# A Perceiver-style network on one core: the second block's convolution, running means and perceptron in four interleaved parts

## The chip, the cores and the metric

The kernel runs on one core of a Trainium2 chip. Five engines work side by side, each through its own queue in order: TensorE (PE, matmuls, with its weight loads PEld), VectorE (DVE), ScalarE (ACT), GpSimd (POOL) and SyncE (SP, which here issues transfers). The metric is the device time of one launch in microseconds (us), as the median of several runs. Everything is float32.

## The reference

Sixteen sequences of 64 positions and 256 features pass through four layers; each adds three parts to x: a cross-attention to a context, a mixer, and a feed-forward part. The change lies in the second layer (L1), from the mixer to the start of the feed-forward part:

```python
x = x + _L1_xattn_ref(_layernorm(x), ctx_768, ...)
x = x + _L1_attn_ref(_layernorm(x), ...)
x = x + _L1_ffn_ref(_layernorm(x), ...)

# _L1_attn_ref, on its input x
h = _ln(x, ln_conv_g, ln_conv_b)
x = x + causal_conv(h, conv_w, K=4, groups=4) + conv_b
h = _ln(x, ln_attn_g, ln_attn_b)
q, k, v = h @ Wq.T + bq, h @ Wk.T + bk, h @ Wv.T + bv
scale = arange(1, S + 1)
pooled_q = cumsum(q, axis=1) / scale
pooled_k = cumsum(pooled_q * k, axis=1) / scale
x = x + pooled_k * v
h = _ln(x, ln_boom_g, ln_boom_b)
h = gelu(h @ Wb.T + bb) @ Wu.T + bu          # 256 -> 1024 -> 256
return x + h

# _L1_ffn_ref: top-1 of 8 experts, 256 -> 1024 -> 256
probs = softmax(x @ router_W + router_b)
gates = one_hot(argmax(probs)) * probs
y = relu(x @ W1[e] + b1[e]) @ W2[e] + b2[e]
out = einsum('bse,besd->bsd', gates, y)
```

## The kernel before

The 1024 rows of x stay in `xs` as eight tiles of 128 rows (tokens) by 256 features. Layers run one after another; a scheduler orders the instructions of each engine when the program is built, except where `manual_schedule` keeps an engine in the order of the text. Each layer opens pools of its own for SBUF (`lp`) and PSUM (`ps_misc` for `misc()`, `lps` for larger tiles); a tile waits until the memory that it takes over is free. Weights are loaded on SP into a ring of two slots: `pack()` hands out the weights of the current step and starts the load of the next (`ahead`).

A normalisation of a tile (`norm_tile`, L150 to L161) takes statistics, aggregate and variance plus epsilon on DVE, the power -1/2 on POOL (L160), and is applied on DVE (L170). `norm` does it for all eight tiles and hands each to `transposed` (two PE transposes into one PSUM tile, L179) and to `put`, which evicts to the features-first layout.

`L1_attn` (L1473) runs stage by stage over all eight tiles: `norm_x` makes `htok` (tokens) and `hT` (features; this one is not read here); a second norm with its own scale and shift goes to the padded `hp` (L1487); the convolution is four shifted matmuls for each of two feature halves and two column halves of 512 (evicted on ACT, L1502); `add_by_features` transposes back and adds (L1511, L1514); a norm into `hT` (L1521); then for each column half and feature half the three projections into PSUM tiles of 512 columns, one buffer for each of q, k, v, and the running means on DVE as scans with a product by 1/position (L1540, L1541, L1555, L1557); added back; a third norm; POOL adds the result to `xs` (L1565); the perceptron for each column half as eight matmul groups of 512 columns with GELU on ACT (L1572), and per tile nine matmuls of 256 columns, the last with the bias row, added to `xs` by `add_to_x` (L89).

`L1_ffn` (L1347) normalises `xs` again (`norm_x`), writes the eight `htok` tiles to DRAM (`hs`, by `keep_row` on SP), makes router logits for all tiles into one PSUM tile, and routes all tiles in one call of `route`: softmax, largest expert, rank of each token among those of its expert (`ranks`: a running count `seen`, two matmuls), one-hot rows and columns for the table of tokens (L1118, L1120, one matmul each), gates. `blocks` turns the counts into up to 15 blocks of 128 tokens of one expert: `rows` (rows of the expert's weights, L1263) and `tokens`. After that call the text adds the gated expert biases `b2` tile by tile (a transpose of the gates, an eviction, one matmul, `add_to_x`). Each block gathers its weights (`wa`, `wb`, 1 MB each) and its token rows (`hb`) by indirect transfers that POOL issues (L1304), three blocks ahead, and runs two matmul groups (`ph`, `po`). The block count is read by all engines after four blocks.

The cross-attention before (`L1_xattn`) and the one after are unchanged.

Of the kernel before, what the change touches and what calls it, by code (L numbers as in the profile page):

```python
# [20 lines left out]
T = B * S  # L21
# [4 lines left out]
E = 8  # L26
# [16 lines left out]
class Net:  # L43
# [4 lines left out]
    def __init__(self, tc, a):  # L48
        self.tc, self.nc, self.a = tc, tc.nc, a
        self.flip = 0  # L50
        self.n_pT = 2
        self.spare_dve = False
        self.halves = None
        self.sb = None
        self.routed = None
# [957 lines left out]
    def gate(self, name, n=NT):  # L1013
        return (self.sb or self.lp).tile([128, n, E], F32, name=name)

    def over_experts(self, x, op, name, out=None):
        n = x.shape[1]
        r = (self.sb or self.lp).tile([128, n], F32, name=name) if out is None else out
# [61 lines left out]
    def keep_row(self, i):  # L1080

        self.nc.sync.dma_start(self.hs[1 + i * 128 : 1 + (i + 1) * 128], self.htok[:, i, :])

    def route(self, r, logits, first, weighed=None, among_chosen=False):
# [18 lines left out]
        at = pool.tile([128, k, n], F32, name="s_at")  # L1103
# [5 lines left out]
        row = pool.tile([128, k, n], F32, name="s_row")  # L1109
# [220 lines left out]
    def pack_L1_gate(self):  # L1330
        self.slot()
        w, row = self.load("L1f_rW"), self.load_row("L1f_rb")
        b2 = self.carve(E, D)
        self.nc.sync.dma_start(b2, self.a["L1f_b2"])
        return w, row, b2

# [10 lines left out]
    def L1_ffn(self):  # L1347
        nc = self.nc
        rw, rb, b2 = self.pack()
        self.norm_x()  # L1350
        self.routed = r = self.route_setup(1)
        for i in range(NT):
            self.keep_row(i)
        gates = self.gate("gates")
        for _ in self.route(r, self.gate_logits(rw, rb), 0, gates):
            pass
        self.rows, self.tokens = self.blocks(r, L1_BLOCKS)
        for i in range(NT):
            pg = self.misc([E, 128])
            nc.tensor.transpose(pg, gates[:, i, :], self.ident)  # L1360
            gT = self.lp.tile([E, 128], F32, tag="gT", bufs=2, name="gT")
            self.evict(gT, pg)
            po = self.misc([128, D])
            self.mm(po, [(gT, b2)])
            self.add_to_x(i, po)
# [103 lines left out]
    def pack_L1_boom(self):  # L1469
        self.slot()  # L1470
        return self.load("L1a_WbT"), self.load("L1a_WuT"), self.load_row("L1a_bu")

    def L1_attn(self):  # L1473
        nc = self.nc
        cv, wq, wk, wv = self.pack()
        self.norm_x()
        h0 = self.htok

        def work(i):
            return self.lp.tile([128, D], F32, tag="lnw", bufs=2, name="lnw")  # L1480

        hp = self.lp.tile([128, 2, B, S + 3], F32, name="hp")
        nc.gpsimd.memset(hp[:, :, :, 0:3], 0.0)

        def put_padded(i, ps):
            for c in range(2):
                nc.vector.tensor_scalar(  # L1487
                    hp[:, c, 2 * i : 2 * i + 2, 3:], ps[:, c, :].rearrange("p (b s) -> p b s", s=S),
                    self.col("L1a_lcg", c), self.col("L1a_lcb", c), ALU.mult, ALU.add,
                )  # L1490

        self.norm(h0, 1e-5, work, put_padded)
        x1 = self.lp.tile([128, NT, D], F32, name="x1")
        conv = self.lp.tile([128, 2, T], F32, tag="res", name="conv")
        for half in range(2):
            for c in range(2):
                ps = self.lps.tile([128, 512], F32, tag="hid", bufs=2, name="ps_conv")
                self.mm(
                    ps.rearrange("p (b s) -> p b s", s=S),
                    [(cv[:, c, k, :], hp[:, c, half * 8 : half * 8 + 8, k : k + S]) for k in range(4)],  # L1500
# [805 lines left out]
```

## Time and profile before

| what | value |
|---|---|
| median of 3 runs (lowest, highest) | 3026.73 us (3026.29, 3029.28) |
| the profiled execution | 3029.32 us, span 3027.5 us |
| PE busy in the span | 2704.1 us (89%) |
| DVE, ACT, POOL busy | 1482.0, 1022.6, 309.4 us |
| mean granted TensorE clock | 0.942 |
| 998.44 to 1189.40: PE, DVE, ACT, POOL busy | 152.48, 96.67, 23.32, 32.35 of 190.96 us |
| granted clock there | 0.82 |

A busy PE is not one at its peak: matmuls are pipelined and their ends are modelled. A float32 matmul shows as two records (passes). The granted clock is the share of TensorE's full clock that was granted in a stretch. An engine's busy share over the whole span mixes stages with different limits; what a change in one stage is worth is read in that stage.

### The profile page before, as it was taken

Reading aid. Unit: us, or ns where it says so; the run is one execution under the profiler, and the core shown is the slowest. Engines: PE = TensorE matmul, PEld = TensorE weight load, DVE = VectorE, ACT = ScalarE, POOL = GpSimd, SP = SyncE. Lnnn points to the kernel's source line nnn. Section 1 sums busy time; section 2 is a strip of 40 time slices with the busy share of each in tenths; the row PEclk is TensorE's granted clock in tenths of the full one; section 3 lists DMA queues with packets and bytes.
Section 4 is the critical chain, followed back from the end, with each engine's and each line's share of the span. In section 5 each row is a group of like instructions: output and inputs, shape, how many; then the busy total and the mean of one; then the engine's idle time right before and its main releaser. Section 6 shows DMA issues by size and latency. Waiting matters only on the chain.

```text
span 3027.5 us, 42618 instructions
## 1 busy us (share of the span) xinstructions
PE 2704.1 (89%) x16840; PEld 1955.0 (65%) x16840; DVE 1482.0 (49%) x3177; ACT 1022.6 (34%) x2290; POOL 309.4 (10%) x428
## 2 busy tenths in 40 slices
PE   7888997999999787979999997887998898887899
PEld 3566784666666346857777776874766666665668
DVE  3654115666666643234444344223445657658581
ACT  2331122555555111223333321122335455455330
POOL 1112223000000112310101011201001000000000
PEclk9997997999999897989999998998999999998999
DMA  9504771101010004811111113450212212121110
GB/s 242 171 27 159 253 230 51 36 26 36 26 36 22 28 9 171 281 49 54 55 44 47 60 42 116 163 217 22 67 43 84 74 51 83 56 67 53 57 36 7
DMA packets 79220, 253.55 MB, mean 84 GB/s; under 512 B 15151, under 2 KB 26954, under 8 KB 69290
## 3 DMA queue, kind: packets, MB, share of 16 engines
q1 hardware_dynamic: 59562, 165.01, 17.5%
q0 software_dynamic: 13312, 80.28, 7.8%
q10 hardware_dynamic: 6144, 5.51, 0.5%
q8 instruction: 134, 2.20, 0.3%
q14 instruction: 68, 0.56, 0.1%
HBM read 233.80 MB, written 14.82 MB: 82 GB/s over the span
## 4 chain that ended last, share of the span: by engine, by line
PE 64%; DVE 11%; ACT 4%; DMA 3%; issue 3%; POOL 1%; SPq 1%; ACTq 0%; DVEq 0%; POOLq 0%
PE misc L69 11%; PE sc L500 8%; PE halves L69 7%; PE gu L69 5%; PE misc L235 4%; PE ps_h L69 4%; PE po L69 4%; PE ps_t L235 3%; PE sc L69 2%; PE misc L864 2%; ACT p L225 2%; PE o L915 2%; PE misc L878 2%; DMA back<-ys,route_at 2%; DVE x L1926 2%
## 5 line engine op out<-in xcount | busy, mean ns | idle before, releaser
L223 DVE TENSOR_REDUCE nmx<-sc 128x1 f32<-128x1024 f32 x264 | 311.6, 1218 | 234.9 <-PE sc L500 150.4
L225 ACT ACTIVATE p<-sc,nmx 128x1024 f32<-128x1024 f32 x264 | 294.6, 1116 | 312.1 <-DVE nmx L223 311.4
L500 PE MATMUL sc<-ctxT,qp 128*128 128x512 f32 (+1 forms) x1024 | 353.4, 599 | 0.0
L500 PEld LDWEIGHTS sc<-ctxT,qp 128*128 128x128 f32 (+1 forms) x1024 | 137.8, 189 | 153.0 <-issue 151.6
L69 PE MATMUL halves<-ctx,pT 128*128 128x192 f32 x1024 | 191.0, 343 | 9.4 <-DVE xs L89 4.0
L69 PEld LDWEIGHTS halves<-ctx,pT 128*128 128x128 f32 x1024 | 178.4, 203 | 12.3 <-DVE xs L89 4.5
L160 POOL TENSOR_TENSOR ln_rs<-ln_ve,nhalf 128x1 f32<-128x1 f32 x120 | 67.0, 563 | 1142.3 <-DVE ln_ve L158 1081.6
L69 PE MATMUL misc<-ctx,pT 128*128 128x192 f32 x1024 | 177.6, 327 | 0.5 <-DVE qT L465 0.5
L69 PEld LDWEIGHTS misc<-ctx,pT 128*128 128x128 f32 x1024 | 166.3, 191 | 2.1 <-DVE qT L465 1.0
L235 PE MATMUL ps_t<-ident,p 128*128 128x128 f32 x1088 | 147.2, 277 | 21.9 <-ACT p L225 14.0
L1916 ACT ACTIVATE da<-rep,al 128x252 f32<-128x252 f32 x256 | 114.7, 498 | 115.0 <-DVE x L1926 95.6
L1926 DVE TENSOR_TENSOR_SCAN x<-da,x 128x512 f32<-128x512 f32 x128 | 151.9, 1210 | 1.9 <-ACT da L1916 1.4
L235 PE MATMUL misc<-ident,p 128*128 128x128 f32 x1024 | 139.8, 283 | 14.1 <-ACT p L225 6.7
L237 ACT COPY pT<-ps_t 128x512 f32<-128x512 f32 x182 | 104.3, 585 | 139.3 <-PE ps_t L235 137.3
L235 PEld LDWEIGHTS ps_t<-ident,p 128*128 128x128 f32 x1088 | 127.1, 143 | 36.0 <-ACT p L225 17.7
L235 PEld LDWEIGHTS misc<-ident,p 128*128 128x128 f32 x1024 | 112.2, 143 | 40.2 <-ACT p L225 13.3
L69 PE MATMUL ps_h<-r,w 128*128 128x256 f32 x512 | 115.3, 385 | 0.0
L237 ACT COPY pT<-misc 128x512 f32<-128x512 f32 x128 | 75.0, 586 | 114.9 <-PE misc L235 114.6
L69 PEld LDWEIGHTS ps_h<-r,w 128*128 128x128 f32 x512 | 97.8, 192 | 16.6 <-issue 2.9
L69 PE MATMUL gu<-dT,wa 128*128 128x128 f32 (+1 forms) x864 | 104.7, 280 | 3.7 <-ACT dT L64 2.4
L239 DVE COPY pT<-misc 128x512 f32<-128x512 f32 x128 | 88.2, 689 | 39.4 <-PE misc L235 28.9
L69 PE MATMUL po<-wb,hid 128*128 128x256 f32 (+1 forms) x440 | 105.9, 388 | 0.2 <-ACT hid L1380 0.2
(468 smaller groups left out, 4449.5 us busy)
## 6 DMA issues: line engine op xcount, KB each, us to landing
ctx<-in_ctx SPq DMA_DIRECT2D x48, 768.0 KB
ctxT<-in_ctxT SPq DMA_DIRECT2D x48, 512.0 KB
w<-in_L2f_W SPq DMA_DIRECT2D x24, 1024.0 KB
rep<-dus SPq DMA_DIRECT2D x256, 64.0 KB
ctxT<-in_ctxT SPq DMA_DIRECT2D x16, 768.0 KB
ctxT<-in_ctxT SPq DMA_DIRECT2D x96, 128.0 KB
ys<-yb ACTq DMA_DIRECT2D x40, 128.0 KB
bc_rep<-bcs SPq DMA_DIRECT2D x32, 128.0 KB
```

Source lines behind the costliest of these rows:

```text
L69: self.nc.tensor.matmul(out, lhsT, rhs, start=n == 0, stop=n == len(pairs) - 1)
L160: nc.gpsimd.tensor_tensor(rs, ve, self.nhalf, ALU.pow)
L223: self.nc.vector.tensor_reduce(nmx, sc, AX.X, ALU.max, negate=True)
L225: self.nc.scalar.activation(p, sc, AF.Exp, bias=nmx, accum_out=sums)
L235: self.nc.tensor.transpose(ps[:, u, :], p[:, at : at + 128], self.ident)
L237: self.nc.scalar.copy(pT[:, 4 * g : 4 * g + 4, :], ps)
L239: self.nc.vector.tensor_copy(pT[:, 0:4, :], ps)
L500: nc.tensor.matmul(sc[u][:, bass.ts(kh, 512)], qp[n][par][rows, h : h + 2, :].rearrange("p h q -> p (h q)"), ctx[0][rows, at], start=n == ...
L864: nc.tensor.matmul(ps[kh], wk[:, kh, cols], cT[:, bass.ts(kh, 512)], start=True, stop=False)
L878: nc.tensor.matmul(ps[kh][:, u, :], cT[:, 512 * kh + at : 512 * kh + at + 128], wv[:, 0, :], start=u == 0, stop=False,)
L1916: nc.scalar.activation(da[:, g, :, 1:], now[j][:, 0, :].rearrange("p (b s) -> p b s", s=S)[:, :, 1:], AF.Exp, scale=al[:, col : col + 1],)
L1926: nc.vector.tensor_tensor_scan(flat, da.rearrange("p g b s -> p (g b s)"), flat, 0.0, ALU.mult, ALU.add)
```

## The change

The mixer and the routing of the next layer are written as one generator `part(p)` for two tiles (256 columns), in four parts that take turns: each `yield` ends a piece, and the loop at the end runs one piece of each part in turn, with PE kept in that order. All matmuls that had 512 columns have 256. The unread `hT` of the first norm is gone. Projections are evicted to SBUF on ACT (q, k and v, with their biases) ahead of the products on DVE, which work in place. Every small matmul result goes through `misc()`, with eight PSUM buffers in this layer. Each part then normalises its tiles, stores their rows, makes its logits and routes its two tiles (the running count goes from part to part), and adds its gated expert biases; `blocks` comes after all of that. The router's weights and `b2` are loaded with the perceptron's; the next layer's weights (L2x) are started at the end of the stage. Small routing tiles get four buffers.

The added functions in full, with the removed text of `L1_attn` left out:

```diff
@@ -51,7 +51,7 @@
         self.n_pT = 2
         self.spare_dve = False
         self.halves = None
-        self.sb = None
+        self.sb, self.gate_bufs = None, 1
         self.routed = None
 
 
@@ -1011,11 +1011,11 @@
         return ps
 
     def gate(self, name, n=NT):
-        return (self.sb or self.lp).tile([128, n, E], F32, name=name)
+        return (self.sb or self.lp).tile([128, n, E], F32, bufs=self.gate_bufs, name=name)
 
     def over_experts(self, x, op, name, out=None):
         n = x.shape[1]
-        r = (self.sb or self.lp).tile([128, n], F32, name=name) if out is None else out
+        r = (self.sb or self.lp).tile([128, n], F32, bufs=self.gate_bufs, name=name) if out is None else out
         self.nc.vector.tensor_reduce(r, x, AX.X, op)
         return r, r.unsqueeze(2).to_broadcast([128, n, E])
 
@@ -1077,9 +1077,9 @@
             row.rearrange("p (d o) -> p d o", o=1), self.lanes[:1, :1].unsqueeze(1).to_broadcast([1, D, 1])
         )
 
-    def keep_row(self, i):
-
-        self.nc.sync.dma_start(self.hs[1 + i * 128 : 1 + (i + 1) * 128], self.htok[:, i, :])
+    def keep_row(self, i, x=None):
+        self.nc.sync.dma_start(self.hs[1 + i * 128 : 1 + (i + 1) * 128], self.htok[:, i, :] if x is None else x)
 
     def route(self, r, logits, first, weighed=None, among_chosen=False):
 
@@ -1100,13 +1100,13 @@
         rank()
 
         k = len(masks)
-        at = pool.tile([128, k, n], F32, name="s_at")
+        at = pool.tile([128, k, n], F32, bufs=self.gate_bufs, name="s_at")
         for m, to in zip(masks, (at[:, x] for x in range(k))):
             t = self.gate("s_t", n)
             nc.vector.tensor_tensor(t, place, self.region.unsqueeze(1).to_broadcast([128, n, E]), ALU.add)
             nc.vector.tensor_tensor(t, t, m, ALU.mult)
             self.over_experts(t, ALU.add, "", to)
-        row = pool.tile([128, k, n], F32, name="s_row")
+        row = pool.tile([128, k, n], F32, bufs=self.gate_bufs, name="s_row")
         nc.vector.tensor_scalar(row, at, 63.5, 1.0 / 128, ALU.subtract, ALU.mult)
         nc.vector.tensor_scalar(row, row, 12582912.0, None, ALU.add)
         nc.vector.tensor_scalar(row, row, 12582912.0, None, ALU.subtract)
@@ -1327,13 +1327,6 @@
         self.nc.scalar.copy(yb, po)
         self.nc.scalar.dma_start(self.ys[j * 128 : (j + 1) * 128, :], yb)
 
-    def pack_L1_gate(self):
-        self.slot()
-        w, row = self.load("L1f_rW"), self.load_row("L1f_rb")
-        b2 = self.carve(E, D)
-        self.nc.sync.dma_start(b2, self.a["L1f_b2"])
-        return w, row, b2
-
     def L1_block(self, j, own=""):
         w = self.lp.tile([128, 2 * 1024 + 8], F32, tag="wa" + own, bufs=1 if own else 3, name="wa")
         self.gather_rows(w, self.a["L1f_W1b"], self.rows[:, j : j + 1])
@@ -1346,23 +1339,8 @@
 
     def L1_ffn(self):
         nc = self.nc
-        rw, rb, b2 = self.pack()
-        self.norm_x()
-        self.routed = r = self.route_setup(1)
-        for i in range(NT):
-            self.keep_row(i)
-        gates = self.gate("gates")
-        for _ in self.route(r, self.gate_logits(rw, rb), 0, gates):
-            pass
-        self.rows, self.tokens = self.blocks(r, L1_BLOCKS)
-        for i in range(NT):
-            pg = self.misc([E, 128])
-            nc.tensor.transpose(pg, gates[:, i, :], self.ident)
-            gT = self.lp.tile([E, 128], F32, tag="gT", bufs=2, name="gT")
-            self.evict(gT, pg)
-            po = self.misc([128, D])
-            self.mm(po, [(gT, b2)])
-            self.add_to_x(i, po)
+        self.rows, self.tokens = self.blocks(self.routed, L1_BLOCKS)
         def block(j, own=""):
             w1, b1, w2 = self.L1_block(j, own)
             dT = self.block_tokens(j, own)
@@ -1468,115 +1446,175 @@
     def pack_L1_boom(self):
         self.slot()
...
+        boom = self.load("L1a_WbT"), self.load("L1a_WuT"), self.load_row("L1a_bu")
+        gate = self.load("L1f_rW"), self.load_row("L1f_rb")
+        b2 = self.carve(E, D)
+        self.nc.sync.dma_start(b2, self.a["L1f_b2"])
+        return boom, gate, b2
     def L1_attn(self):
         nc = self.nc
...
+        (cv, *qkv), ((wb, wu, bu), (rw, rb), b2) = self.pack(), self.pack(ahead=False)
+        self.lps_close()
+        routed, self.gate_bufs = self.route_setup(1), 4
+        later = self.later_steps(CHUNK)
+        def tokens(p, name):
+            return self.lp.tile([128, 2, D], F32, name=f"{name}{p}")
+        def features(p, name):
+            return self.lp.tile([128, 2, CHUNK], F32, name=f"{name}{p}")
+        def normalized(src, out):
+            for t in range(2):
+                mv, rs = self.norm_tile(src(t), 1e-5)
+                nc.vector.tensor_scalar(out[:, t, :], src(t), mv[:, 0:1], rs, ALU.subtract, ALU.mult)
+        def affine(x, t, to, g, b):
+            ps = self.transposed(x[:, t, :])
             for c in range(2):
...
+                nc.vector.tensor_scalar(to(c), ps[:, c, :], self.col(g, c), self.col(b, c), ALU.mult, ALU.add)
+        def added(x, to):
+            for t in range(2):
                 ps = self.misc([128, D])
                 for c in range(2):
...
+                    nc.tensor.transpose(ps[:, c * 128 : (c + 1) * 128], x[:, c, t * 128 : (t + 1) * 128], self.ident)
+                nc.vector.tensor_tensor(to[:, t, :], to[:, t, :], ps, ALU.add)
+        def part(p):
+            tiles = (2 * p, 2 * p + 1)
+            hp = self.lp.tile([128, 2, 4, S + 3], F32, name=f"hp{p}")
+            nc.gpsimd.memset(hp[:, :, :, 0:3], 0.0)
+            x1, w = tokens(p, "x1"), tokens(p, "lnw")
+            normalized(lambda t: self.xs[:, tiles[t], :], x1)
+            normalized(lambda t: x1[:, t, :], w)
+            yield
+            for t in range(2):
+                ps = self.transposed(w[:, t, :])
                 for c in range(2):
                     nc.vector.tensor_scalar(
...
+                        hp[:, c, 2 * t : 2 * t + 2, 3:], ps[:, c, :].rearrange("p (b s) -> p b s", s=S),
+                        self.col("L1a_lcg", c), self.col("L1a_lcb", c), ALU.mult, ALU.add,
                     )
...
+            yield
+            ps = self.misc([128, 2, CHUNK])
+            conv = features(p, "hTs")
+            for c in range(2):
+                self.mm(
+                    ps[:, c, :].rearrange("p (b s) -> p b s", s=S),
+                    [(cv[:, c, k, :], hp[:, c, :, k : k + S]) for k in range(4)],
                 )
...
+            for c in range(2):
+                nc.scalar.activation(conv[:, c, :], ps[:, c, :], AF.Identity, bias=self.col("L1a_conv_b", c))
+            yield
+            added(conv, x1)
+            w = tokens(p, "lnw")
+            normalized(lambda t: x1[:, t, :], w)
+            yield
+            hT = features(p, "hTs")
+            for t in range(2):
+                affine(w, t, lambda c: hT[:, c, t * 128 : (t + 1) * 128], "L1a_lag", "L1a_lab")
+            yield
+            q, k, v = (features(p, name) for name in "qkv")
+            for m, x, name in zip(qkv, (q, k, v), "qkv"):
+                ps = self.misc([128, 2, CHUNK])
+                for o in range(2):
+                    self.mm(ps[:, o, :], [(m[:, c, o * 128 : (o + 1) * 128], hT[:, c, :]) for c in range(2)])
+                for o in range(2):
+                    nc.scalar.activation(x[:, o, :], ps[:, o, :], AF.Identity, bias=self.col(f"L1a_b{name}", o))
+                if name != "k":
+                    yield
+            inv = self.inv_s.unsqueeze(1).unsqueeze(1).to_broadcast([128, 2, 4, S])
+            def running_mean(x):
+                for c in range(2):
+                    nc.vector.tensor_tensor_scan(x[:, c, :], later, x[:, c, :], 0.0, ALU.mult, ALU.add)
+                steps = x.rearrange("p c (b s) -> p c b s", s=S)
+                nc.vector.tensor_tensor(steps, steps, inv, ALU.mult)
+            running_mean(q)
+            nc.vector.tensor_tensor(q, q, k, ALU.mult)
+            running_mean(q)
+            nc.vector.tensor_tensor(v, v, q, ALU.mult)
+            yield
+            yield
+            added(v, x1)
+            w = tokens(p, "lnw")
+            normalized(lambda t: x1[:, t, :], w)
+            for t in range(2):
+                x = self.xs[:, tiles[t], :]
+                nc.gpsimd.tensor_tensor(x, x, x1[:, t, :], ALU.add)
+            yield
+            hT = features(p, "hTs")
+            for t in range(2):
+                affine(w, t, lambda c: hT[:, c, t * 128 : (t + 1) * 128], "L1a_lbg", "L1a_lbb")
+            yield
+            if p < 2:
+                g = self.act.tile([128, 8, CHUNK], F32, tag=("htok", "hT")[p], name="hid")
+            else:
+                g = self.lp.tile([128, 8, CHUNK], F32, name=f"hid{p}")
+            for m2 in range(4):
+                ps = self.misc([128, 2, CHUNK])
+                for u in range(2):
+                    m = 2 * m2 + u
+                    self.mm(ps[:, u, :], [(wb[:, c, m * 128 : (m + 1) * 128], hT[:, c, :]) for c in range(2)])
+                for u in range(2):
+                    m = 2 * m2 + u
+                    nc.scalar.activation(g[:, m, :], ps[:, u, :], AF.Gelu, bias=self.col("L1a_bb", m))
+                if m2 == 1:
+                    yield
+            yield
+            for t in range(2):
                 po = self.misc([128, D])
                 self.mm(
                     po,
                     [(g[:, m, t * 128 : (t + 1) * 128], wu[:, m, :]) for m in range(8)] + [(self.ones[:1, :], bu)],
                 )
...
+                self.add_to_x(tiles[t], po)
+                yield
+            o = tokens(p, "x1")
+            normalized(lambda t: self.xs[:, tiles[t], :], o)
+            for t in range(2):
+                self.keep_row(tiles[t], o[:, t, :])
+            yield
+            hT = features(p, "hTs")
+            for t in range(2):
+                self.evict(hT[:, :, t * 128 : (t + 1) * 128], self.transposed(o[:, t, :]))
+            yield
+            ps = self.misc([128, 2, E])
+            for t in range(2):
+                self.mm(
+                    ps[:, t, :],
+                    [(hT[:, c, t * 128 : (t + 1) * 128], rw[:, c, :]) for c in range(2)] + [(self.ones[:1, :], rb)],
+                )
+            gates = self.gate(f"gates{p}", 2)
+            for _ in self.route(routed, ps, tiles[0], gates):
+                yield
+            yield
+            gTs = []
+            for t in range(2):
+                pg = self.misc([E, 128])
+                nc.tensor.transpose(pg, gates[:, t, :], self.ident)
+                gTs.append(self.lp.tile([E, 128], F32, tag="gT", bufs=8, name="gT"))
+                self.evict(gTs[t], pg)
+            yield
+            for t in range(2):
+                po = self.misc([128, D])
+                self.mm(po, [(gTs[t], b2)])
+                self.add_to_x(tiles[t], po)
+            yield
+        with self.tc.manual_schedule(engines={mybir.EngineType.PE}):
+            parts = [part(p) for p in range(NC)]
+            while parts:
+                parts = [p for p in parts if next(p, parts) is not parts]
+        self.start_pack(self.at)
+        self.routed, self.gate_bufs = routed, 1
@@ -2110,7 +2148,7 @@
             "L0_ffn": (self.L0_ffn, []),
             "L1_xattn": (self.L1_xattn, [self.pack_L1_xattn]),
             "L1_attn": (self.L1_attn, [self.pack_L1_attn, self.pack_L1_boom]),
-            "L1_ffn": (self.L1_ffn, [self.pack_L1_gate]),
+            "L1_ffn": (self.L1_ffn, []),
             "L2_xattn_attn": (self.L2_xattn_attn, [lambda: self.pack_heads64("L2"), self.pack_L2_attn]),
             "L2_ffn": (self.L2_ffn, [self.pack_L2_gate] + [lambda e=e: self.pack_L2_expert(e) for e in range(E)]),
             "L3": (None, [lambda: self.pack_heads64("L3"), self.pack_L3_attn, self.pack_L3_ffn]),
@@ -2127,7 +2165,7 @@
                 if name == "L0_first" else nullcontext() as sb,
                 tc.tile_pool(name=f"sb_{name}", bufs=1, side=side, reuse_waits="tile") as self.lp,
                 tc.tile_pool(
-                    name=f"psm_{name}", bufs=3 if name == "L1_xattn" else 2, space=PSUM, reuse_waits="tile"
+                    name=f"psm_{name}", bufs={"L1_xattn": 3, "L1_attn": 8}.get(name, 2), space=PSUM, reuse_waits="tile"
                 ) as self.ps_misc,
             ):
                 self.sb = sb
```

## The prediction

> **What bounds the kernel now.** I read the page's chain that ended last, then the busy times cut into the stages that the change touches, then the timeline where stages meet.
>
> ```profile
> span 3027.5 us, 42618 instructions
> PE 64%; DVE 11%; ACT 4%; DMA 3%; issue 3%; POOL 1%; SPq 1%; ACTq 0%; DVEq 0%; POOLq 0%
> ```
>
> PE sets most of the end, yet the second block is not one thing. The busy times by stage (columns: length, busy time and instructions of each engine, granted clock, DMA):
>
> ```profile
> core 0: us, PE busy (x) PEld busy (x) DVE busy (x) ACT busy (x) POOL busy (x), PEclk, DMA share, GB/s
> 998.44:1010.00 11.56, 5.43 (x24) 2.69 (x24) 9.85 (x39) 1.49 (x4) 3.30 (x6) 0.77 0.48 182
> 1010.00:1027.60 17.60, 17.23 (x40) 7.89 (x41) 5.16 (x20) 2.06 (x3) 1.65 (x3) 0.86 0.00 1
> 1027.60:1039.40 11.80, 5.58 (x28) 3.06 (x27) 10.14 (x37) 0.69 (x1) 2.71 (x5) 0.83 0.00 0
> 1039.40:1067.70 28.30, 24.52 (x61) 10.39 (x60) 25.78 (x46) 4.03 (x5) 2.18 (x4) 0.95 0.00 1
> 1067.70:1081.10 13.40, 5.32 (x20) 2.75 (x21) 10.24 (x37) 0.00 (x0) 7.67 (x13) 0.57 0.00 1
> 1081.10:1096.50 15.40, 15.40 (x40) 7.07 (x39) 5.32 (x20) 4.81 (x7) 1.62 (x3) 0.93 0.00 1
> 1096.50:1144.40 47.90, 47.90 (x177) 31.97 (x175) 11.27 (x36) 6.19 (x9) 4.11 (x8) 1.00 0.06 21
> 1144.40:1158.80 14.40, 12.64 (x65) 11.16 (x64) 3.11 (x10) 2.77 (x5) 0.55 (x1) 0.74 0.47 159
> 1158.80:1172.20 13.40, 5.71 (x22) 4.64 (x22) 10.63 (x58) 0.26 (x1) 0.00 (x0) 0.50 0.00 1
> 1172.20:1189.40 17.20, 12.74 (x27) 5.16 (x27) 5.16 (x23) 1.02 (x4) 8.56 (x9) 0.50 0.87 319
> ```
>
> In order: the convolution's normalisation, convolution, second normalisation, projections with running means, third normalisation, perceptron (two rows), router logits, routing, gated biases. The normalisations belong to DVE, the perceptron to PE (47.90 of 47.90). Two things matter here. PE begins each matmul phase when half of its tiles are ready (conv at 1010, projections at 1039.4), the other transposes lying between its matmuls. And the last row is not waste: 319 GB/s of expert weights flow under it.
>
> One normalisation, in the timeline (start, length, engine, line):
>
> ```profile
> 1101.26 0.43 DVE L154 BATCH_NORM_STATS2 ln_st<-xs 128x6 f32<-128x256 f32 x1
> 1101.72 0.18 DVE L156 BATCH_NORM_AGGREGATE ln_mv<-ln_st 128x2 f32<-128x6 f32 x1
> 1101.94 0.15 DVE L158 TENSOR_SCALAR ln_ve<-ln_mv 128x1 f32<-128x1 f32 x1
> 1102.24 0.55 POOL L160 TENSOR_TENSOR ln_rs<-ln_ve,nhalf 128x1 f32<-128x1 f32 x1 [17.04 <-DVE ln_ve L158]
> 1102.82 0.41 DVE L170 TENSOR_SCALAR htok<-xs,ln_mv,ln_rs 128x256 f32<-128x256 f32 x1 [0.73 <-POOL ln_rs L160]
> ```
>
> From the variance on DVE, through POOL's power, to the application: 1102.82 - 1101.94 = 0.88 us that other DVE work must fill.
>
> **The change, part by part.** The sum goes against the profiled execution (span 3027.5, 3029.3 in all), which is 2.6 above the median 3026.7. The order in which the changed kernel is built has PE walk whole rounds: the transposes of parts 0 to 3, then the convolutions of parts 0 to 3, and so on. DVE is ordered by the scheduler, and its row order is known. I price that order with DVE paces of back-to-back rows: application 0.32, statistics 0.33, aggregate 0.09, variance 0.06, affine eviction 0.33.
>
> *First normalisation.* Both norms of all eight tiles now stand behind the preceding cross-attention; before, six applications ran under it (PE there 99.7 to 100 busy of each 100 us, so freeing them there gains nothing). A part's turn on DVE is 4 applications, 4 statistics, 4 aggregates, 4 variances, 2 evictions: 1.28 + 1.32 + 0.36 + 0.24 + 0.66 = 3.86; each application waits a further 0.34 or so for POOL (0.88 less the 0.5 of rows that the order puts in between), 5.24. Lead 0.93 + three turns of 5.24 + a last one of 3.57 + 0.65 for transposes = 20.9, and only then may the first convolution start, since PE's queue holds it behind part 3's transposes. Before: 11.6. **+9.3.** Gone are the 16 transposes and 8 evictions into hT, which lay in the first 4 us.
>
> *Convolution.* 64 passes of 256 columns at 0.214 (perceptron rows: 16 in 3.62, hence 16 of 4.27 with the bias row) = 13.7, plus a slow start. The first expert block's 32 passes took 6.33 against 3.84 for the next: 2.5 lost, at a granted clock of 0.50. So 16.2 against 17.6: **-1.4.** Matmuls of half the width cost nothing by themselves, as the weight loads (0.19 to 0.20) hide under 0.214; without that cover the perceptron's 128 passes alone would cost 25 more.
>
> [...]
>
> *Second normalisation.* Eight tiles of add 0.33, statistics, aggregate, variance, application = 1.13 each, 9.0; three affine evictions 1.0; POOL waits 0.5 a tile, 4.1; ends 1.1: 15.2. Before, 11.8, since the first projection went after four tiles. **+3.4.**
>
> *Projections and means.* First q 3.4 (slow clock) + ACT and hand-over 1.1; DVE means 4 x 1.9 (two half-length scans of 1.22/2 and a 0.69 product) = 7.6; then 4 x 3.1 = 12.4, and two adds 0.7: 25.2, PE's 20.6 under it. Before 28.3 (PE waited for its PSUM buffers). **-3.1.**
>
> *Third normalisation.* As the second, 15.3, because POOL's eight residual adds (0.73 each, L1565) now lie between its powers, for +2, while some work has already run. Before 13.4. **+1.9.**
>
> *Perceptron.* 27.4 + 8 x 4.27 + 2.5 = 64.1 against 63.3. **+0.8.** The running sum at the last perceptron matmul is +10.9.
>
> *From there to the first expert matmul*, before: 1190.52 - (1143.73 + 0.69) = 46.1.
>
> ```profile
> 1171.98 0.23 DVE L1263 TENSOR_SCALAR rows<-of,lane 128x15 int32<-128x15 f32 x1
> 1172.49 1.00 POOL L1304 DMA_INDIRECT wa<-in_L1f_W1b,rows  x1 [25.68 <-DVE first L1278]
> 1190.52 6.33 PE L69 MATMUL ph<-dT,wa 128*128 128x128 f32 x32 [0.46 <-ACT dT L64]
> 1201.04 3.84 PE L69 MATMUL ph<-dT,wa 128*128 128x128 f32 x32 [0.52 <-DVE dT L62]
> ```
>
> After: last tile's norm and transposes 5.1; logits 9.9 as before; then in DVE's order the maxima of parts 2 and 3 stand first, so all routing follows part 3's logits. It has 85 small operations (before, some 26), 16 one-hot rows at 0.21 and four table adds at 0.3: 85 x 0.13 + 3.4 + 1.2 + 1.0 of PE round trips = 16.6. (0.13: thirteen interleaved rows from 1171.71 to 1173.31.) Gate transposes 0.7. The eight bias matmuls, 2 x 0.43 at half clock, 0.9 each: 7.2. They now stand in PE's queue ahead of the block count, so count 0.9 and rows 2.0 come after them, and the gathers begin with nothing left to cover them. Of their latency no row is direct: the windows show 243, 366, 360, 201 GB/s over 2 us each from 1174, so block 0's 2.23 MB are in by 1181.5, 9.3 after the rows; +0.2. Sum 51.9. **+5.8.** The 14 blocks at 8.0 are unchanged: three are gathered ahead, and one follows each finished block.
>
> *Queues.* On SP the three router loads move ahead to the perceptron's weights, then come L2x's five (held until the projections free their slot), then eight row stores, 0.33 to 0.43 each to issue: all are out some 30 us before the gather that reads the rows. L2a's five loads wait for the slot that the bias matmuls free, with the block count's load behind them on SP; it is needed only after four blocks. Their 0.64 MB meet the first gather, 1.5 at 427 GB/s, which the gather's upper bound holds. On POOL the block gathers stand behind nothing but the residual adds and powers, long done.
>
> [...]
>
> Sum: 10.9 + 5.8 = 16.7; 3046.0 for the profiled execution, **3043** as a median.
>
> Bounds of what no row shows: routing pace 0.06 (variance row) to 0.26 (dependent row), -6/+11; POOL wait per normalisation 0.2 to the full 0.88 over 32 of them, -9/+13; bias matmuls 0.43 (full clock) to 1.22 (as measured), -4/+3; logits all fast or all slow, -3/+2; gather 7.0 (427 GB/s, the best window, after 1.8 of silence) to 14.8 (sharing with block 1), -2/+6; three slow starts at 1.2 to 3.5 each, -4/+3. I take the values nearest to rows of the same stage.
>
> **The rivals.** *The parts overlap in earnest (faster):* in my count PE idles about 36 us before the perceptron (15.6, 10, 10 in the three norms). If DVE's work on one part really hides under PE's on another, and two thirds of that go, 24, the time is 3043 - 24 = 3019. It decides from 17 hidden microseconds on. For: 1010 to 1027.6 shows both engines working so. Against: PE's fixed rounds and the DVE sum, which even without stalls fills the norms.
>
> *POOL's wait stays bare (much slower):* +13, 3056. For: 0.73 idle before L170 in the rows above. Against: four chains to interleave.
>
> *Tail no longer than before:* full clock in logits and biases (-7), gather at 7.0 (-2), a few short routing rows (-2): 3032, no clear change. Against: 0.50 granted all through 1158.8 to 1189.4.
>
> *The parts don't take turns:* DVE's order could have put part after part; it alternates, so this has no share.
>
> **How the numbers follow.** Forecast 61%, bare wait 15%, unchanged tail 14%, overlap 10%. A difference under 0.2%, 6 us, can't be told from none. Faster 9%, all of it overlap; same 11%, mostly the unchanged tail; slower 80%. The bounds, which seldom fall all on one side, give about -13/+15, and the range takes in the bare wait and half of the unchanged tail: 3029 to 3058.
>
> **What would show it.** Right: first convolution at about 1019 and last perceptron matmul at about 1155 in the profile; PE idle over 8 us ahead of each matmul phase; the first gather after the last bias matmul, and PE idle some 9 us behind it. Wrong: convolution before 1012, a granted clock near 1.0 in the norms, or weights moving before the bias matmuls.

## The result and the profile after

The changed kernel is slower. Its median is 3041.11 us over 20 runs (3034.94 to 3046.49); the kernel before, run beside it, has 3028.52 over 20 (3021.72 to 3039.17). The ratio is 1.0039, with a 95% interval of 1.0030 to 1.0048: some 12 us, with 9 to 14.5 inside the interval. The profiled execution took 3038.85 us, 9.5 more than that of before.

The first row of the changed kernel's chain that ended last:

```profile
PE 63%; DVE 11%; issue 4%; ACT 4%; DMA 4%; POOL 2%; SPq 1%; ACTq 0%; DVEq 0%; POOLq 0%
```

Against before, PE has one point less of the chain, and GpSimd, DMA and "issue" (where no releaser is seen) have one more each. That is a hint and no more; the stages tell it. Busy times of the changed kernel, cut at the same events as before the change (columns: length, busy time and instructions of each engine, granted clock, DMA share, GB/s):

```profile
core 0: us, PE busy (x) PEld busy (x) DVE busy (x) ACT busy (x) POOL busy (x), PEclk, DMA share, GB/s
998.92:1019.20 20.28, 5.26 (x17) 2.52 (x18) 16.12 (x72) 0.00 (x0) 7.60 (x14) 0.50 0.28 105
1019.20:1035.00 15.80, 15.80 (x65) 13.44 (x65) 2.00 (x7) 2.52 (x6) 0.00 (x0) 0.87 0.01 1
1035.00:1049.80 14.80, 6.50 (x33) 3.96 (x32) 11.21 (x46) 0.84 (x2) 4.40 (x8) 0.68 0.00 0
1049.80:1076.40 26.60, 24.29 (x110) 20.93 (x108) 24.61 (x47) 11.36 (x25) 1.61 (x2) 0.92 0.09 36
1076.40:1092.20 15.80, 5.76 (x21) 2.96 (x22) 11.74 (x45) 0.00 (x0) 9.12 (x15) 0.55 0.20 74
...
1155.30:1170.00 14.70, 13.02 (x65) 12.40 (x64) 3.53 (x14) 3.12 (x7) 0.81 (x2) 0.65 0.05 15
1170.00:1183.20 13.20, 9.68 (x42) 7.13 (x41) 12.11 (x109) 1.23 (x6) 0.00 (x0) 0.50 0.00 1
1183.20:1187.10 3.90, 3.90 (x18) 3.10 (x17) 3.17 (x8) 0.13 (x1) 0.00 (x0) 0.94 0.00 0
1187.10:1190.20 3.10, 0.55 (x3) 0.45 (x2) 2.84 (x19) 0.00 (x0) 0.00 (x0) 0.50 0.51 140
1190.20:1200.60 10.40, 0.66 (x3) 0.55 (x3) 0.91 (x8) 0.00 (x0) 7.68 (x9) 0.50 0.89 291
```

In order: first normalisation, convolution, second normalisation, projections and means, third normalisation; then, past the perceptron, logits, routing, gated biases, block count, first gather. The first row holds most of the loss: 20.3 us where before had 11.6. In the three rows of normalisations PE is busy 5.26, 6.50 and 5.76 of 20.28, 14.80 and 15.80, so it idles for 15.0 + 8.3 + 10.0 = 33 us there, where before had 6.1 + 6.2 + 8.1 = 20. The last row is PE idle under a gather that moves 291 GB/s.

Inside the second normalisation, DVE's timeline of the changed kernel (start, length, engine, line, operation, and in brackets the idle time before it with its releaser):

```profile
1043.17 0.13 DVE L158 TENSOR_SCALAR ln_ve<-ln_mv 128x1 f32<-128x1 f32 x1
1043.23 0.41 DVE L1487 TENSOR_TENSOR x<-x,misc 128x256 f32<-128x256 f32 x1
1044.04 0.41 DVE L1473 TENSOR_SCALAR lnw<-x,ln_mv,ln_rs 128x256 f32<-128x256 f32 x1 [0.40 <-POOL ln_rs L160]
...
1045.64 0.41 DVE L1473 TENSOR_SCALAR lnw<-x,ln_mv,ln_rs 128x256 f32<-128x256 f32 x1 [0.40 <-POOL ln_rs L160]
```

A tile takes 1.60 us (1044.04 to 1045.64), and 0.40 of it is the wait for GpSimd's power, tile after tile: DVE's order puts one row (0.41) between a variance and the application that needs it, and the round trip takes 0.87 (1043.17 to 1044.04).

The stretch runs from the last attention matmuls (ym) to the first expert matmul (ph). PE's timeline where it begins, in the kernel before and then in the changed one:

```profile
995.93 1.99 PE L69 MATMUL misc<-w,ym 128*128 128x256 f32 x8 [0.78 <-DVE ym L943]
995.26 3.13 PE L69 MATMUL misc<-w,ym 128*128 128x256 f32 x8 [0.78 <-DVE ym L943]
```

and in the changed kernel at its end:

```profile
1183.18 3.96 PE L69 MATMUL misc<-w,gT 8*128 8x256 f32 x16
1187.07 0.58 PE L69 MATMUL misc<-route_seen,ones 128*128 128x8 f32 x2
1190.92 0.61 PE L69 MATMUL misc<-at_block,route_table 64*128 64x15 f32 x2 [3.27 <-DVE back_r L1019]
1200.55 0.69 PE L179 MATMUL misc<-ident,hb 128*128 128x128 f32 x2 [9.03 <-DMA hb<-hs,tokens]
1201.76 6.61 PE L69 MATMUL ph<-dT,wa 128*128 128x128 f32 x32 [0.52 <-ACT dT L64]
```

The eight biases stand ahead of the block count and take 3.96; then nothing covers the gather, and PE waits 9.03 us. What stands ahead of this block starts some microseconds earlier or later in each execution, so from here on I compare one length: from the start of the attention's last group of matmuls (ym, 995.93 before and 995.26 after) to ph. Before: 1190.52 - 995.93 = 194.6. After: 1201.76 - 995.26 = **206.5**. The difference, 11.9, is nearly all of the loss that the medians show (12.6). 1.1 of it lies in ym itself, whose eight passes were granted a clock of 0.61 instead of 1.00 (they took 3.16 to 3.36 in e1, e3 and e4 too, and 1.99 in the other runs); why is not shown. Outside the stretch single executions differ by more than that: the span less the length is 2832.9 before, 2829.3 after, and 2825 to 2845 in the runs below.

### The profile page after: what moved, and what is told of

Same layout as the page of the kernel before. It is cut to its first block, busy times and chain, and to the rows that moved or that the text cites. A ratio compares the mean times of both kernels' runs of the same rounds, so it can differ in the third digit from the quotient of the medians.

```text
span 3035.8 us, 43038 instructions
## 1 busy us (share of the span) xinstructions
PE 2699.5 (89%) x16980; PEld 1983.4 (65%) x16980; DVE 1482.7 (49%) x3247; ACT 1032.3 (34%) x2329; POOL 310.3 (10%) x431
## 4 chain that ended last, share of the span: by engine, by line
PE 63%; DVE 11%; issue 4%; ACT 4%; DMA 4%; POOL 2%; SPq 1%; ACTq 0%; DVEq 0%; POOLq 0%
PE misc L69 12%; PE sc L500 8%; PE halves L69 7%; PE gu L69 5%; PE misc L235 4%; PE ps_h L69 4%; PE po L69 4%; PE ps_t L235 3%; PE sc L69 2%; PE misc L864 2%; PE o L915 2%; ACT p L225 2%; PE misc L878 2%; DVE x L1964 2%; DMA back<-ys,route_at 2%
## 5 line engine op out<-in xcount | busy, mean ns | idle before, releaser
L235 PE MATMUL misc<-ident,p 128*128 128x128 f32 x1024 | 138.3, 280 | 13.4 <-ACT p L225 6.3
L69 PEld LDWEIGHTS ps_h<-r,w 128*128 128x128 f32 x512 | 97.8, 192 | 16.6 <-issue 2.9
## 6 DMA issues: line engine op xcount, KB each, us to landing
ctxT<-in_ctxT SPq DMA_DIRECT2D x16, 768.0 KB, 12.7
```

The costliest lines, as they stand in the source:

```text
L69: self.nc.tensor.matmul(out, lhsT, rhs, start=n == 0, stop=n == len(pairs) - 1)
L235: self.nc.tensor.transpose(ps[:, u, :], p[:, at : at + 128], self.ident)
```

## The experiments

Theory: the loss is made in the normalisations. They lost the cover of the cross-attention, and in lockstep every matmul phase waits for all eight tiles, whose work on DVE carries a bare wait for GpSimd each. The tail is even, since what the routing saved went into an uncovered gather. Rivals: fixed rounds on PE cost it whatever DVE does; the waits only fill time; the gather ends when it ends.

| run | what is done | ratio to before (95%) | ym to ph, us | against the changed kernel |
|---|---|---|---|---|
| changed kernel | | 1.0039 (1.0030 to 1.0048) | 206.5 | |
| e1 | biases after the block count | 1.0017 (1.0002 to 1.0032) | 202.3 | -4.2 |
| e2 | first normalisation under the attention | 1.0007 (0.9993 to 1.0021) | 198.2 | -8.3 |
| e3 | statistics, then applications | 0.9953 (0.9936 to 0.9969) | 186.2 | -20.3 |
| e4 | parts two turns apart | 0.9960 (0.9945 to 0.9974) | 186.7 | -19.8 |
| e5 | kernel before, statistics then applications | 0.9994 (0.9981 to 1.0006) | 195.3 | (+0.7 on before) |
| e6 | e1, e2 and e3 | 0.9937 (0.9917 to 0.9957) | 178.0 | -28.5 |
| e7 | e6, two turns apart | 0.9907 (0.9889 to 0.9924) | 169.1 | -37.4 |
| e8 | e6, three turns apart | 0.9905 (0.9887 to 0.9924) | 165.3 | -41.2 |

Each length is read from one execution. By the medians the gains over the changed kernel come out larger by 1 to 6 us in e1 to e7 (about 26 for e3, 24 for e4), which is within about the width of the intervals.

### The biases after the block count

```diff
-                gTs.append(self.lp.tile([E, 128], F32, tag="gT", bufs=8, name="gT"))
-                self.evict(gTs[t], pg)
-            yield
-            for t in range(2):
-                po = self.misc([128, D])
-                self.mm(po, [(gTs[t], b2)])
-                self.add_to_x(tiles[t], po)
+                self.evict(self.gTs[:, tiles[t]], pg)
 ...
         self.rows, self.tokens = self.blocks(self.routed, L1_BLOCKS)
+        for i in range(NT):
+            po = self.misc([128, D])
+            self.mm(po, [(self.gTs[:, i, :], self.b2)])
+            self.add_to_x(i, po)
+        self.start_pack(self.at)
```

> The gated biases are added after the block count again, under the first gather of expert weights. Theory (the biases stand on the path and the gather has nothing over it): the gather begins 3.9 earlier (the biases' 1183.18 to 1187.14), they run inside the 9 us in which PE is idle, first expert matmul about 1198 in the profile instead of 1201.8, and the whole about 4 us faster than the changed kernel, ratio to before about 1.0026. Rival (the first gather is limited by what else flows, so it ends when it ends): the first expert matmul stays near 1201, ratio 1.004.

PE's timeline of this run:

```profile
1190.63 0.44 PE L69 MATMUL misc<-route_seen,ones 128*128 128x8 f32 x2
1194.43 0.42 PE L69 MATMUL misc<-at_block,route_table 64*128 64x15 f32 x2 [3.37 <-DVE route_at L1284]
1194.79 7.38 PE L69 MATMUL misc<-w,gTs 8*128 8x256 f32 x16
1203.99 0.66 PE L179 MATMUL misc<-ident,hb 128*128 128x128 f32 x2 [1.82 <-DMA hb<-hs,tokens]
1205.11 5.33 PE L69 MATMUL ph<-dT,wa 128*128 128x128 f32 x32 [0.46 <-ACT dT L64]
```

The block count now comes first, the biases run inside the gather, and PE waits 1.82 for it instead of 9.03. The length is 4.2 shorter, about the 3.9 that the biases took on the path. (The attention ended 7.5 later in this execution, so the expected "about 1198" is read from the length.) The biases themselves are slower, 7.38 instead of 3.96 for the same 16 passes, behind 3.37 us in which PE idled; in the cover that costs nothing, since PE still waits the 1.82 behind them. The gather gained nothing from having less beside it. In the changed kernel five loads of the next layer (L2a, 0.64 MB) are issued from 1187.17 to 1190.1 and flow beside its start; here they stand behind the biases, which end at 1202.17 (1194.79 + 7.38). From the block count's matmul to the transposes of block 0's tokens 9.6 us pass in both.

### The first normalisation back under the attention

```diff
+        x0 = self.act.tile([128, NT, D], F32, tag="htok", name="x1")
 ...
-            x1, w = tokens(p, "x1"), tokens(p, "lnw")
+            x1, w = x0[:, 2 * p : 2 * p + 2, :], tokens(p, "lnw")
 ...
-            if p < 2:
-                g = self.act.tile([128, 8, CHUNK], F32, tag=("htok", "hT")[p], name="hid")
+            if p == 1:
+                g = self.act.tile([128, 8, CHUNK], F32, tag="hT", name="hid")
 ...
-            o = tokens(p, "x1")
+            o = tokens(p, "lnw")
```

> The first normalisation writes into the buffer that it had before, which is free while the cross-attention still runs. Theory (8 to 9 us of the loss come from this normalisation no longer running under the cross-attention): first convolution near 1011 instead of 1019.2, about 8 us faster than the changed kernel, ratio to before about 1.0012. Rival (the fixed rounds of PE cost it, the cover does not matter): convolution still after 1016, at most 3 us gained, ratio 1.003 to 1.004.

The last attention group and the convolution in PE's timeline of this run:

```profile
994.66 1.99 PE L69 MATMUL misc<-w,ym 128*128 128x256 f32 x8 [0.78 <-DVE ym L943]
...
1009.78 16.17 PE L69 MATMUL misc<-hp,w 128*128 128x256 f32 x64
```

It starts 1009.78 - 994.66 = 15.1 after the start of the last attention group, against 1019.18 - 995.26 = 23.9 in the changed kernel and 14.1 before. Of the 8.8 gained here, 7.7 lie behind the end of ym (20.8 to 13.1) and 1.1 in ym's own matmuls. The order on PE is unchanged, so the fixed rounds alone do not cost this; moving the buffer takes it away. One choice of memory gave up the cover: in the changed kernel the tiles that x's normalisation writes come from the block's own pool, and no application into them ran before the attention's last addition.

### Statistics of all parts, then applications

```diff
-            for t in range(2):
-                mv, rs = self.norm_tile(src(t), 1e-5)
+            got = [self.norm_tile(src(t), 1e-5) for t in range(2)]
+            yield
+            for t, (mv, rs) in enumerate(got):
                 nc.vector.tensor_scalar(out[:, t, :], src(t), mv[:, 0:1], rs, ALU.subtract, ALU.mult)
```

(`normalized` becomes a generator, called with `yield from`, and `ln_mv` and `ln_rs` get eight buffers.)

> Each normalisation becomes two pieces: the statistics of all four parts, then the applications of all four, so that GpSimd's power has the other parts' statistics to hide under. Theory (0.40 us of bare wait before each application, on 32 of them, is on the path): 8 to 11 us faster than the changed kernel, the three normalisations about 16, 12 and 13 long instead of 20.3, 14.8 and 15.8, ratio to before 1.0003 to 1.0013. Rival (the wait only fills time that DVE spends waiting for transposes or PE anyway): at most 3 us, ratio above 1.003.

Busy times of this run, cut at the same events (first normalisation, convolution, second normalisation, projections, third normalisation):

```profile
997.65:1008.92 11.27, 3.45 (x17) 2.99 (x17) 11.11 (x50) 0.00 (x0) 5.94 (x9) 0.67 0.49 188
1008.92:1022.92 14.00, 14.00 (x66) 12.17 (x66) 4.08 (x14) 2.52 (x6) 0.00 (x0) 1.00 0.01 1
1022.92:1033.33 10.41, 5.35 (x33) 4.75 (x32) 10.10 (x44) 0.84 (x2) 4.89 (x8) 0.79 0.00 0
1033.33:1059.80 26.47, 24.06 (x113) 20.72 (x112) 25.67 (x51) 11.36 (x25) 2.24 (x2) 0.95 0.13 45
1059.80:1070.20 10.40, 4.56 (x17) 2.43 (x17) 9.56 (x39) 0.00 (x0) 8.55 (x14) 0.50 0.24 89
```

The three normalisations take 11.3, 10.4 and 10.4 where 20.3, 14.8 and 15.8 stood (the first row begins 0.45 us earlier in the hand-over from the attention than the changed kernel's row), and DVE is busy 11.11 of 11.27 in the first: bare work, no holes. The gain is twice what I expected, and beats the kernel before. Inside these three rows the idle time that applications spend on GpSimd falls from 10.9 us to 0.4, 10.5 of the 18.8 gained. The rest is work that now lies elsewhere: 22 DVE instructions fewer inside the first stage (72 to 50) and six fewer inside the third (45 to 39). In the first stage fifteen of them belong to the statistics of x for five tiles, which no longer queue behind an application that waits, and so ran under the attention (six tiles there instead of one); six are evictions into hp, which now run under the convolution. The convolution, too, is 1.8 shorter, at a granted clock of 1.00 instead of 0.87; in this run sixteen transposes in one piece (3.45 us) stand directly ahead of it. It starts 14.6 after ym with the buffer of the changed kernel, so this order alone takes away what e2 takes away by the buffer. The edit also gives the statistics eight buffers instead of four, as the order needs; the buffers without the order were not run.

### Parts two turns apart

```diff
-            while parts:
-                parts = [p for p in parts if next(p, parts) is not parts]
+            for turn in range(60):
+                for p in range(NC):
+                    if turn >= 2 * p:
+                        next(parts[p], None)
```

> Part p starts 2p turns after part 0, so that the parts stand in different pieces, nothing else changed. Theory (lockstep puts all eight tiles of a normalisation ahead of every matmul phase; PE is idle about 33 us in the three of them): PE has matmuls of one part beside the normalisation of another, 15 to 25 us faster than the changed kernel, ratio to before 0.9955 to 0.999. Rival (DVE and the hand-overs between three engines set the pace whatever the order; the tail gets longer as the last part routes alone): no more than 5 us either way, ratio 1.002 to 1.006.

PE's timeline of this run where the parts lie across each other:

```profile
1041.57 0.69 PE L179 MATMUL misc<-ident,lnw 128*128 128x128 f32 x2 [0.95 <-DVE lnw L1473]
1042.05 6.37 PE L69 MATMUL misc<-hTs,w 128*128 128x256 f32 x16
1048.25 0.60 PE L179 MATMUL misc<-ident,lnw 128*128 128x128 f32 x4
1048.69 3.62 PE L69 MATMUL misc<-hp,w 128*128 128x256 f32 x16
1052.15 0.60 PE L1486 MATMUL misc<-ident,v 128*128 128x128 f32 x4
...
1057.53 0.44 PE L179 MATMUL misc<-ident,lnw 128*128 128x128 f32 x2 [2.62 <-DVE ln_ve L158]
```

Projections (hTs), a convolution (hp) and transposes of means (v) of different parts now stand side by side, and the transposes at 1048.25 found their normalisation done. Waits of 1 to 2.6 us remain, the power's 0.40 among what makes them. Up to the last perceptron matmul the length is 15.9 shorter (144.2 instead of 160.1), and the tail behind it 3.9, since the first two parts' routing lies among the perceptron matmuls of the others. The rounds on PE are a cost, then, as they are: with them undone much of the normalisations hides, though DVE's order and its waits for GpSimd stay.

### The control: the same order in the kernel before

```diff
-        for i in range(NT):
-            mv, rs = self.norm_tile(src[:, i, :], eps)
+        got = [self.norm_tile(src[:, i, :], eps) for i in range(NT)]
+        for i, (mv, rs) in enumerate(got):
             o = out(i)
```

(for the three normalisations inside the block, the same eight buffers)

> The kernel before, with its three normalisations inside the second block (not the one of x ahead of them) taken as statistics of all eight tiles first and applications after. Theory (the bare wait for GpSimd is a cost of the order on DVE, in both kernels; in the kernel before its trace shows 5.5 us of it ahead of these 24 applications): 3 to 6 us faster than before, ratio 0.998 to 0.999. Rival (in the kernel before the statistics of late tiles keep the first half of the tiles from being ready early, so the matmul phases start later): 1.000 to 1.003.

No change can be told from none, and the interval (0.9981 to 1.0006) does not exclude my theory's 0.998 to 0.999; the trace speaks against it. Groups of DVE instructions from 998 to 1145, first of the kernel before (columns: instructions; busy us and mean ns; idle us before them, and what ended it):

```profile
L1521 DVE TENSOR_SCALAR hT<-misc,vecs 128x128 f32<-128x128 f32 x32 | 11.3, 403 | 1.2 <-PE misc L179 0.7
L170 DVE TENSOR_SCALAR lnw<-x,ln_mv,ln_rs 128x256 f32<-128x256 f32 x16 | 6.9, 434 | 4.6 <-POOL ln_rs L160 4.4
```

and then of this run:

```profile
L1530 DVE TENSOR_SCALAR hT<-misc,vecs 128x128 f32<-128x128 f32 x32 | 11.0, 404 | 6.7 <-PE misc L188 6.7
L179 DVE TENSOR_SCALAR lnw<-x,ln_mv,ln_rs 128x256 f32<-128x256 f32 x16 | 6.0, 404 | 0.0
```

The 4.6 us ahead of the applications are gone, and 5.5 more stand ahead of the evictions, now waiting for PE's transposes. The length is 195.3 against 194.6: 0.9 shorter up to the last perceptron matmul (147.6 against 148.5), 1.6 longer in the tail, which the edit does not touch. The rival's reason did not come either: from ym's start the convolution begins at 14.2 (14.1 before), the projections at 43.2 (43.4), the perceptron at 83.0 (85.2). So a bare wait for GpSimd need not be a cost wherever it is seen; in this run most of it only changed its place. That this is because PE may begin a phase with half of the tiles, and that in lockstep it costs because PE may not begin before the last tile, fits e3 and e5 but no run separates it from the rest of the two kernels' differences.

### All of it together

The three edits of the first runs in one kernel (the transposed gates take the buffer that x's normalisation leaves), in lockstep, then with the parts two and three turns apart:

> The first three edits together (biases after the block count, first normalisation under the attention, statistics before applications), parts in lockstep. Theory: the gains add except where the second and third both shorten the first normalisation (11.3 left of it): 20.5 + 4 + 1 to 5, ratio 0.993 to 0.9955. Rival (the gains share one bound, such as DVE's own work ahead of the convolution, and do not add): ratio 0.995 to 0.997.

> The three edits together and the parts two turns apart. Theory (PE's idle time in the norms is now DVE's bare work, about 11 + 10 + 10 us; staggered parts hide a good part of it, and the routing of early parts runs under later perceptrons): a further 8 to 18 below the lockstep version, ratio 0.988 to 0.992. Rival (with the waits gone the two remedies cover the same idle time, and staggering adds a routing of the last part alone at the end): no better than the lockstep version, ratio 0.993 to 0.996.

> As the run before with the parts three turns apart. Theory: the first part's lead over the last grows from 6 to 9 turns, more of the norms hidden but a longer run-out at the end: within 4 us of two turns apart, ratio 0.987 to 0.992. Rival (the run-out decides): 5 to 10 us slower than two turns apart.

In lockstep the length falls by 28.5, where the single gains sum to 32.8; the overlap is in the first normalisation, which two of the edits shorten (the convolution starts 11.0 after ym, against 15.1 in e2, 14.6 in e3 and 23.9 in the changed kernel). Staggering takes a further 8.9 and 12.7. The last is 29.3 below before in length, and 0.9905 of its time, about 29 us. Two and three turns can't be told apart (the intervals lie on each other), and the rival for three, a longer run-out, did not come. What is left is that run-out: what PE waits for in the last run from 985 to 1170 (columns: total us, times, longest):

```profile
PE misc L69 <- DVE route L1043: 7.3, 3, 3.7
PE misc L69 <- DVE s_col L1118: 4.3, 2, 2.2
PE misc L179 <- DVE lnw L1479: 3.4, 2, 2.4
PE misc L69 <- DVE route_at L1284: 3.4, 1, 3.4
```

Three of these four are routing; the normalised tiles hold 3.4 here, and further rows have 3.3 for hp and 1.1 for hTs, which are made from them. In the changed kernel the same view has 19.2 + 9.2 + 5.4 for the transposes of normalised tiles:

```profile
PE misc L179 <- DVE ln_ve L158: 19.2, 7, 3.6
PE misc L179 <- DVE ln_mv L156: 9.2, 9, 1.5
PE misc L179 <- DMA hb<-hs,tokens: 9.0, 1, 9.0
PE misc L179 <- DVE lnw L1473: 5.4, 8, 1.6
```

## Why the prediction was right, and where it was not

The side and the cause were right, and the signs named for it came: first convolution at 1019.18, last perceptron matmul at 1154.65, PE idle 15.0, 8.3 and 10.0 ahead of the matmul phases and 9.03 behind the gather's start; the granted clock in the normalisations was 0.50 to 0.68. Step by step, predicted and measured:

| step | before | predicted | measured |
|---|---|---|---|
| first normalisation | 11.6 | 20.9 | 20.3 |
| convolution | 17.6 | 16.2 | 15.8 |
| second normalisation | 11.8 | 15.2 | 14.8 |
| projections and means | 28.3 | 25.2 | 26.6 |
| third normalisation | 13.4 | 15.3 | 15.8 |
| perceptron | 63.3 | 64.1 | 63.1 |
| sum to its last matmul, against before | | +10.9 | +10.4 |
| logits, with the norm ahead | | 15.0 | 14.6 |
| routing | | 16.6 | 12.5 |
| gate transposes | | 0.7 | 0.8 |
| bias matmuls | | 7.2 | 4.0 |
| count and rows | | 2.9 | 2.6 |
| gather to first ph | | 9.5 | 12.0 |
| tail | 46.1 | 51.9 | 46.4 |

To the measured +10.4 come the 1.1 of ym, which no step has, and the tail's 0.3: 11.9.

**First normalisation.** Right in size and mechanism: moved back under the attention (e2), it gave 7.7 of the 8.7 back. What the prediction took for 0.34 of wait per application is 0.40.

**Lockstep.** Predicted 36 us of idle PE in the normalisations, measured 33. The rival of parts that overlap in earnest had no place in this order, as argued; e4, where the order allows it, shows its size: 15.9 up to the last perceptron matmul, against the 24 of that rival.

**Half-width matmuls.** Nothing by themselves: the perceptron took 63.1 against 63.3 (the convolution's row of before also holds transposes, so 15.8 against 17.6 says less).

**The tail is the step that failed**, by size and not by mechanism: +5.8 predicted, +0.3 measured. Two terms were too dear. The *routing* was priced at 0.13 a small operation, from thirteen interleaved rows of before, among them two that read 120 columns and three that read 64. DVE's timeline of the changed kernel:

```profile
1171.94 0.17 DVE L1019 TENSOR_REDUCE t_at<-route 128x2 f32<-128x16 f32 x1
1172.02 0.17 DVE L1043 TENSOR_TENSOR route<-route,t_at 128x16 f32<-128x16 f32 x1
1172.10 0.17 DVE L1019 TENSOR_REDUCE t_at<-route 128x2 f32<-128x16 f32 x1
```

With four parts to choose from, one starts every 0.08 us though each lasts 0.17. So 0.13 was too dear, and the routing took 4.1 less than predicted.

The *bias matmuls* were priced at half clock, and the windows grant 0.94 there (3.90 us, busy throughout), after one-hot matmuls and gate transposes had kept PE busy from 1179.45 on without a gap. The third term was too cheap: the *gather* to ph took 12.0 instead of 9.5, of which 1.2 are the transposes and the eviction of block 0's tokens, which the step had left out.

So the rival of an unchanged tail came about as far as the tail goes, by quick routing and a granted clock of 0.94 in the biases, close to what it said. Its total of 3032 did not: it needed 7 us off logits and biases together, where 0.4 and 3.2 came, and a gather of 7.0, where a longer one came. The sum of the steps, +16.7, was 4.8 above the 11.9 measured. That 3043 lies within 2 us of the median is partly luck, since before itself measured 3028.5 beside it and not 3026.7.

**The bare wait** (rival, 3056) was real at 0.40 of the full 0.88 us. By the prediction's own terms (0.34 on sixteen applications, about 0.5 on the other sixteen) its bounds would have been -7 and +15 rather than -9 and +13. What the prediction did not see is that it could be ordered away, and that the reordering which does so is worth more than the change cost.

## What to carry to other kernels

Parts that take turns piece by piece in lockstep are one large part with more instructions: TensorE, kept in the order of the text, still waits for the last tile of each piece (33 us of idling in the three normalisations here). Start them some turns apart, or put the pieces so that a hand-over that is waited for (here the power on GpSimd, 0.40 us ahead of each application) has the other parts' work to hide under. And before a stage is rewritten, note what runs ahead of its time into a buffer that is already free, and keep that buffer.

## What the runs showed of the hardware

- A busy PE did not get its full clock at once. In the changed kernel it was busy 1.64 and 2.00 of the 2 us from 1179 and 1181 at a granted clock of 0.50, and had 0.94 from 1183.2. The sixteen passes of the biases took 3.96 there and 7.38 in e1, behind 3.37 us of idling and without a wait among them (in e6 to e8 7.26 to 7.45 us). Why they took so long is not shown.
- The first expert block's 32 passes took 6.61 in the changed kernel after 9.03 us of idling, at a granted clock of 0.56, and 5.33 in e1 after 1.82. Against the 3.84 of the block that follows it in the kernel before (granted clock 1.00), 2.8 and 1.5 are lost. How long PE idled does not decide it alone: before lost 2.5 (6.33, at 0.59) with no gap over 0.46 us from 1173.53 on, at a granted clock of 0.50 up to its start, and e6 to e8 lost 1.8 to 2.2 after 1.8 to 2.0 us of idling.
- From the first issue of the gather (1190.48) to block 0's transposes 10.1 us passed. In e1 the biases did not slow it: from the block count's matmul to those transposes 9.6, as in the changed kernel (1190.92 to 1200.55), though only in the changed kernel the L2a loads run beside it.
